# A two-layer cross network on one core: VectorE's order in layer 2, and a third buffer for layer 1's kept channels

## The chip, the cores and the metric

The kernel runs on one core of a Trainium2 chip. The metric is device microseconds from the first to the last instruction of one execution, the median of several runs. All data is float32.

## The reference, cut to what matters

```python
ROWS, FIELDS, EMB = 4096, 32, 16

def _batchnorm(h, gamma, beta):            # per channel, over rows and embedding
    mean = jnp.mean(h, axis=(0, 2), keepdims=True)
    var = jnp.var(h, axis=(0, 2), keepdims=True)
    return (h - mean) * jax.lax.rsqrt(var + EPS) * gamma[None, :, None] + beta[None, :, None]

def _cin_layer(out, x, W, b, gamma, beta):
    r, _, e = x.shape
    h = jnp.einsum('rne,rfe->rnfe', out, x).reshape(r, -1, e)   # all products of two fields
    h = jnp.einsum('rce,oc->roe', h, W) + b[None, :, None]      # 128 output channels
    return _batchnorm(h, gamma, beta)

h1 = _cin_layer(x, x, W1, b1, g1, beta1)         # 32 x 32 products
out, direct1 = (h1[:, :64], h1[:, 64:])
direct2 = _cin_layer(out, x, W2, b2, g2, beta2)  # 64 x 32 products
agg = jnp.concatenate([direct1, direct2], axis=1)
return agg.sum(axis=-1)
```

There are 4096 x 16 = 65,536 sites. For each, layer 1 multiplies fields by fields and contracts the products with `W1`; half of its channels are kept for layer 2, the other half goes to the output. Layer 2 multiplies the 64 kept channels by the 32 fields and contracts with `W2`. Batch norm needs statistics of all sites, so layer 2 starts only when layer 1 has ended.

## The kernel before

Sites are taken in tiles of 512 columns, and two tiles make a pair: 128 tiles, 64 pairs. **Layer 1**, tile by tile: VectorE multiplies (`z`), TensorE contracts into a PSUM bank, ScalarE copies the bank out with its bias, VectorE takes statistics. The kept channels of a pair are gathered in a tile `kept` and written to HBM:

```python
opool = one.enter_context(tc.tile_pool(name="opool", bufs=2))
# [...] in finish(t), for each tile t of pair c:
            if half == 0:
                eds[c] = epool.tile([P, T], FP, tag="ed", name="ed")
                kept[c] = opool.tile([KEEP, 2 * T], FP, tag="h", name="kept")
            e = opool.tile([P, T], FP, tag="e", name="e")
            nc.scalar.activation(e, ps, AF.Identity, bias=b1)
            stats1.add(e)
            h = kept[c]
            nc.scalar.activation(h[:, half * T : (half + 1) * T], ps[:KEEP, :], AF.Identity, bias=b1[:KEEP])
            if half == 1:
                nc.scalar.dma_start(hs[c], kept.pop(c))
```

The last two pairs of layer 1 first finish their kept half (L468 is the copy, L470 the statistics), so that the factors of layer 2 are known early; their direct half follows on TensorE behind it:

```python
        for c in range(NC - ENDING // 2, NC):
            add_halves(banks, zs, 0, ks, True, True)           # matmuls of the kept channels
            h = opool.tile([KEEP, 2 * T], FP, tag="h", name="kept")
            for half, k in enumerate(ks):
                # [...] copy out of PSUM on ScalarE, statistics on VectorE
            nc.scalar.dma_start(hs[c], h)
        # [...] mean, variance, root, scale and shift -> keep, by a small matmul into keep_ps
```

**Layer 2** takes a pair c in four stages k (i = 3, 0, 1, 2). In each, ScalarE makes two factors `f` in PSUM (kept channels, scaled and shifted), VectorE multiplies them with the fields `b` and `bx` into `zz`, and GpSimd makes sums `t` of the products. TensorE contracts both: the 2 x 2 blocks of channels and tiles are multiplied in a scheme that saves block products by such sums.

```python
psum = ctx.enter_context(tc.tile_pool(name="psum", bufs=6, space=bass.MemoryType.PSUM))
factors = ctx.enter_context(tc.tile_pool(name="factors", bufs=2, space=bass.MemoryType.PSUM))
z2pool = ctx.enter_context(tc.tile_pool(name="z2pool", bufs=3))   # zz
tpool = ctx.enter_context(tc.tile_pool(name="tpool", bufs=2))     # t
hpool = ctx.enter_context(tc.tile_pool(name="hpool", bufs=1))     # th

def sum_products(z):                     # stages 1 to 3, on GpSimd
    t = tpool.tile([P, 3, 2, T], FP, tag="t", name="t")
    queue("pool", lambda: nc.gpsimd.tensor_tensor(t[:, 0], z[:, 1], z[:, 0], ALU.add))             # L674
    twice = t[:, 0].unsqueeze(1).to_broadcast([P, 2, 2, T])
    queue("pool", lambda: nc.gpsimd.tensor_tensor(t[:, 1:3], z[:, 2:4], twice, ALU.subtract))      # L677
    return t
# sum_half(z, b11), stage 0: th = one add on VectorE, one subtraction on GpSimd (L685)
```

TensorE takes in each stage: `x1`, `x32`, then `x54` of the stage before, then `x67`; in the last stage its own `x54` at the end. `x67` reads t[:, 0], `x54` reads t[:, 1:3]. All matmuls of layer 2 go through line 669, and two of them, for the low and high 64 rows of a PSUM bank, run beside each other. A pair uses four of six banks: x11, x62, x34 and x57. When a pair's matmuls have ended, `combine` adds its banks up during the next pair's stages. It is a generator, and each `step()` records one section of it:

```python
    def combine(c, sums_):
        act(both[low], x11[high]); act(both[high], x11[low], bias=b2[low])      # ScalarE
        yield
        add(both, both, x11)                                                    # VectorE
        yield
        if idle:
            dve(idle.pop(0))              # statistics of layer 1's direct half, in the first pairs
        add(e[:, 0], both, x62)           # VectorE: e0
        yield
        act(u2[low], e[low, 0], ...); act(u2[high], e[low, 0], ...)             # ScalarE
        yield
        add(u3, u2, x57)                                                        # VectorE
        yield
        act(u3_low, u3[high])                                                   # ScalarE
        yield
        add(e[:, 1], u3, x34); add(e[low, 0], u3_low, x57[low])                 # VectorE: e1, e_low
        yield
        # [...] squares on ScalarE; in the first pair statistics on VectorE
        yield
        # [...] tensor_reduce d<-e on VectorE
        yield
```

The stage loop before:

```python
        for k, i in enumerate(STAGES):
            # [...]
            multiply(z[:, 0::3], f1, b)          # VectorE: zz<-f,b
            if k in (1, 2, 3):
                step()
            if c > 0 or k > 0:
                f2 = factor(raw[i], i, 1)        # ScalarE
                if k == 1:
                    step()
                # [...] stage 0: copy b11 on ScalarE
                multiply(z[:, 1:3], f2, bx)      # VectorE: zz<-f,bx
            # [...] t = sum_half(...) in stage 0, sum_products(z) else
            if k == 1:
                step()
            if k < 3:
                f1 = factor(raw[STAGES[k + 1]], STAGES[k + 1], 0)   # ScalarE, for the next stage
            if k == 0:
                step(2)
            if k == 2:
                step()
            # [...]
            if k == 1:
                step()
            # [...] the matmuls of the stage
        steps = combine(c, sums_)
```

VectorE, ScalarE, GpSimd and TensorE each keep the order in which their instructions are recorded here.

Of the kernel before, what the change touches and what calls it, by code (L numbers as in the profile page):

```python
# [38 lines left out]
FP = mybir.dt.float32  # L39
# [8 lines left out]
T = 512  # L48
# [3 lines left out]
KEEP = 64  # L52
# [16 lines left out]
def tile_cin(ctx: ExitStack, tc: tile.TileContext, xa, xb, xr, w1, w1m, w2, bn, out):  # L69
# [119 lines left out]
    def load_x(g, k):  # L189

        at = xb.offset + ((2 * DIFF * g + 1) * WRAP + 2 * k) * T
        nc.sync.dma_start(xs[:, k], bass.AP(xb.tensor, at, [[2 * WRAP * T, DIFF], [4 * T, 8], [1, 2 * T]]))

    def negate(part):
        x = xs[:, 0, part * T : (part + 1) * T]
        return nc.scalar.activation(x, x, AF.Identity, scale=-1.0)

    def difference(part):

        to = slice(part * T // 2, (part + 1) * T // 2)  # L200
        return nc.vector.tensor_reduce(xd[:, to], xs[:, :, to].rearrange("p k t -> p t k"), AX.X, ALU.add)

    def store_difference(g):
        return nc.scalar.dma_start(diffs[g], xd)
# [10 lines left out]
    def loaded(c):  # L215
        if c == 0:
            b, bx, *a = early[-6:]
        else:
            with tc.issue_after(loads[-1].ins):
                b, bx = load_b(c), load_bx(c)  # L220
                a = [load_a(c, i) for i in STAGES]
        return dict(zip(STAGES, a)), b, bx
# [3 lines left out]
    def queue(engine, make):  # L226

        with tc.issue_after(lasts[engine].ins) if engine in lasts else nullcontext():
            lasts[engine] = make()
        return lasts[engine]  # L230
# [30 lines left out]
    with ExitStack() as one:  # L261
        lpool = one.enter_context(tc.tile_pool(name="lpool", bufs=4))
        rpool = one.enter_context(tc.tile_pool(name="rpool", bufs=1))
        opool = one.enter_context(tc.tile_pool(name="opool", bufs=2))
        zpool = one.enter_context(tc.tile_pool(name="zpool", bufs=4))
        wpool = one.enter_context(tc.tile_pool(name="wpool", bufs=1))

# [49 lines left out]
        kept = {}  # L317

        def finish(t):

            c, half = divmod(t, 2)
            ps = pss.pop(t)
            to = slice(half * KEEP, (half + 1) * KEEP)
            if half == 0:
                eds[c] = epool.tile([P, T], FP, tag="ed", name="ed")
                kept[c] = opool.tile([KEEP, 2 * T], FP, tag="h", name="kept")
            ed = eds[c]
            e = opool.tile([P, T], FP, tag="e", name="e")
            nc.scalar.activation(e, ps, AF.Identity, bias=b1)  # L329
# [5 lines that stand above are left out]
            done = nc.scalar.activation(ed[to, :], ps[KEEP:, :], AF.Identity, bias=b1[KEEP:])  # L335
            if half == 1:
                sum_direct(c)
            return done

        def sum_direct(c):  # L340
            return nc.vector.tensor_reduce(
                d1[:, c * RT : (c + 1) * RT],
                eds.pop(c).rearrange("p (r e) -> p r e", e=EMB),
                AX.X,
                ALU.add,
            )
# [81 lines left out]
        def add_halves(banks, zs, direct, ks, begun, ended):  # L428

            for m in range(4):  # L430
                for k in ks:
                    matmul(
                        banks[k][half_of[(k + direct) % 2]],
                        w1_sb[:, m, half_of[direct]],
                        zs[k][:, m // 2, m % 2, :],
                        m == 0 and not begun,
                        m == 3 and ended,
                    )
# [20 lines left out]
        for c in range(NC - ENDING // 2, NC):  # L459
            ks = tuple(2 * c + half - ending for half in range(2))  # L460
            add_halves(banks, zs, 0, ks, True, True)
            h = opool.tile([KEEP, 2 * T], FP, tag="h", name="kept")
            for half, k in enumerate(ks):
                at = half_of[half]
                to = h[:, half * T : (half + 1) * T]
                bias = (b1, b1_swapped)[half][at]
                with tc.issue_after(evicted.ins):
                    queue("act", lambda: nc.scalar.activation(to, banks[k][at], AF.Identity, bias=bias))  # L468
                stats = stats1.more[low, 2 * k : 2 * k + 2].rearrange("p a b -> p (a b)")
                queue("dve", lambda: nc.vector.bn_stats(stats, to))  # L470
            nc.scalar.dma_start(hs[c], h)
# [324 lines left out]
    def step(count=1):  # L796
        for _ in range(count):
            next(steps, None)

    for c in range(NC):  # L800
        raw, b, bx = loaded(c)
        sums_ = Sums()
        g = c // DIFF + 1
        if g < NC // DIFF:
            if c % DIFF == 2:
                with tc.issue_after(loads[-1].ins):
                    for k in range(2):
                        load_x(g, k)
            if c % DIFF == 4:
                for k in range(2):  # L810
                    queue("act", lambda: negate(k))
                idle += [lambda k=k: difference(k) for k in range(4)]
            if c % DIFF == 13:
                queue("act", lambda: store_difference(g))

        f1 = factor(raw[STAGES[0]], STAGES[0], 0)
        for k, i in enumerate(STAGES):

            z = z2pool.tile([P, 4, 2, T], FP, tag="zz", name="zz")
            if c == k == 0:  # L820

                f2 = factor(raw[i], i, 1)
                for q in range(2):
                    multiply_part(z[:, 0::3], f1, b, q)
                    multiply_part(z[:, 1:3], f2, bx, q)
                b11 = factors.tile([P, T], FP, tag="f", name="b11")
                act(b11, z[:, 0, 1])
            else:
                multiply(z[:, 0::3], f1, b)
            if k in (1, 2, 3):  # L830

                step()
            if c > 0 or k > 0:
                f2 = factor(raw[i], i, 1)
                if k == 1:
                    step()
                if i == PLAIN:
                    b11 = factors.tile([P, T], FP, tag="f", name="b11")
                    act(b11, z[:, 0, 1])
                multiply(z[:, 1:3], f2, bx)  # L840

            plain = (0,) if i == PLAIN else (0, 1) if c == 0 and k == 3 else ()
            if i == PLAIN:
                t = sum_half(z, b11)
            elif not plain:
                t = sum_products(z)
            if k == 1:
                step()
            if k < 3:
                f1 = factor(raw[STAGES[k + 1]], STAGES[k + 1], 0)  # L850
            if k == 0:
                step(2)
            if k == 2:

                step()
            for _ in range(min(len(sums_left), 4 if c == NC - 1 else 1)):
                queue("act", sums_left.pop(0))
            if k == 1:
                step()

            low_first = c % 2 == 0
            rest = not low_first
            last = range(8) if k == 3 else ()
            if c == 0 and k > 1:
                last = ((0, 1, 6, 7), (2, 3, 4, 5))[k - 2]
            stage = Stage(sums_, i, z, t, plain, last)
            if i == PLAIN:
                stage.ordinary(low_first, 0)
            if len(plain) == 2:
                stage.ordinary(rest, 0)  # L870
            else:
                stage.x1(low_first if i == PLAIN else rest)
                stage.x32(rest)
            if k > 0:
                waiting.x54(rest)
            if len(plain) == 2:
                stage.ordinary(rest, 1)
            else:
                stage.x67(rest)
                if k == 3:  # L880
                    stage.x54(rest)
            waiting = stage

            if c == 9 and k == 2:
                queue("act", direct_factors)
            if 10 <= c < 14 and k == 2:
                queue("act", lambda: scale_direct(c - 10))
            if c == 15 and k == 2:
                with tc.issue_after(loads[-1].ins):
                    write_direct()  # L890
        steps = combine(c, sums_)
# [90 lines left out]
```

## Time and profile before

| | |
|---|---|
| time, median of 3 runs | 2090.25 us (2089.69 to 2091.75) |
| span of the profiled run | 2088.1 us |
| layer 1 | to 476 us |
| change of layers, first layer 2 pair | 476 to about 520 us |
| layer 2 | to 2071 us, then 17 us to the end |
| one multiplication zz on VectorE | 2.27 us, eight in a pair |
| one first sum t (L674), one second sum (L677) on GpSimd | 2.37 and 4.56 us, three of each in a pair |
| one th sum on GpSimd (L685) | 2.37 us |
| `both`, e, u on VectorE | 0.67 to 0.69 us each |

In the profile, PE is TensorE, PEld its weight loads, DVE VectorE, ACT ScalarE, POOL GpSimd and SP SyncE. A matmul in float32 shows as two records. A wait is written as the engine and line that waited, and what released it. A timeline line gives start, duration, engine, line, operation and tiles; in brackets is the idle time before it and what ended it. Tile names are cut to their stem: `x` stands for the four banks of layer 2, `u` for u2 and u3, `e` for all parts of e. A wait for several things is put down to the one that came last.

### The profile page before, as it was taken

What the parts mean: (1) busy time and instruction counts of PE and PEld (TensorE: products, weight loads), DVE (VectorE), ACT (ScalarE), POOL (GpSimd) and SP (SyncE); (2) the same over time, 40 slices, a digit from 0 to 9 for tenths busy, and PEclk for the clock granted to TensorE, in tenths of its full rate; (3) what the DMA queues carried; (4) which work ended last, traced back from release to release, by engine and by line L of the source; (5) the groups of instructions that cost most, each with busy time, mean ns of one, the idle gap of its engine ahead of it and who ended that gap; (6) DMA issues with size and microseconds to landing.
All of it is one profiled execution on the core that took longest, in us unless ns stands there. A gap on an engine that the chain in (4) does not pass through costs nothing.

```text
span 2088.1 us, 23629 instructions
## 1 busy us (share of the span) xinstructions
PE 2066.8 (99%) x8634; PEld 1024.2 (49%) x8634; DVE 1890.0 (91%) x1391; ACT 1008.3 (48%) x1594; POOL 1472.0 (70%) x453
## 2 busy tenths in 40 slices
PE   9999999999999999999999999999999999999996
PEld 3444444443343555555555555555555555555553
DVE  8998888888999999899999998999999989999996
ACT  4555555554454444445444445454444454444443
POOL 0000000003999999999999999999999999999995
PEclk9999999999999999999999999999999999999998
DMA  9999999997666787776677777766667777667751
GB/s 384 390 335 345 335 363 352 350 337 193 162 168 165 172 195 189 192 176 166 166 188 173 185 174 176 172 169 162 170 168 183 177 174 178 169 165 168 171 142 41
DMA packets 112020, 440.65 MB, mean 211 GB/s; under 512 B 13088, under 2 KB 13088, under 8 KB 103456
## 3 DMA queue, kind: packets, MB, share of 16 engines
q1 hardware_dynamic: 105456, 418.43, 73.3%
q10 hardware_dynamic: 6448, 20.72, 2.6%
q8 instruction: 67, 1.10, 0.2%
q14 instruction: 49, 0.40, 0.1%
HBM read 417.07 MB, written 22.02 MB: 210 GB/s over the span
## 4 chain that ended last, share of the span: by engine, by line
PE 94%; DVE 2%; POOL 1%; issue 1%; DMA 1%; ACT 1%; DVEq 0%; SPq 0%; ACTq 0%; POOLq 0%
PE x L669 72%; PE ps L397 21%; PE ps L358 2%; DVE zz L638 1%; POOL t L677 0%; DMA h<-kept 0%; POOL t L674 0%; DMA b<-in_xb 0%; ACT f L630 0%; DVE zz L643 0%; DVE e L633 0%; ACT both L630 0%; DVE d L912 0%; ACT unread L568 0%; ACT u L630 0%
## 5 line engine op out<-in xcount | busy, mean ns | idle before, releaser
L669 PE MATMUL x<-zz,s_sb 128*64 128x512 f32 x2048 | 946.3, 592 | 0.3 <-DVE zz L638 0.3
L669 PE MATMUL x<-zz,w_sb 128*64 128x512 f32 x2312 | 889.9, 592 | 0.0
L677 POOL TENSOR_TENSOR t<-zz,t 128x2048 f32<-128x2048 f32 x191 | 870.7, 4559 | 15.0
L669 PE MATMUL x<-t,s_sb 128*64 128x512 f32 x1528 | 694.2, 593 | 0.1
L630 ACT ACTIVATE f<-a,keep 128x512 f32<-128x512 f32 x512 | 398.0, 778 | 415.2 <-DVE zz L638 371.5
L638 DVE TENSOR_TENSOR zz<-f,b 128x2048 f32<-128x2048 f32 x255 | 580.6, 2277 | 0.1
L638 DVE TENSOR_TENSOR zz<-f,bx 128x2048 f32<-128x2048 f32 x255 | 579.9, 2274 | 0.0
L674 POOL TENSOR_TENSOR t<-zz 128x1024 f32<-128x1024 f32 x191 | 453.2, 2373 | 89.6 <-DVE zz L638 80.0
L685 POOL TENSOR_TENSOR th<-zz,th 128x1024 f32<-128x1024 f32 x64 | 151.8, 2373 | 487.4 <-DVE th L633 487.3
L397 PE MATMUL ps<-z,w_sb 128*128 128x512 f32 x992 | 434.2, 595 | 0.6 <-DVE z L365 0.6
L669 PEld LDWEIGHTS x<-zz,s_sb 128*64 128x64 f32 x2048 | 279.6, 137 | 228.6 <-issue 159.1
L669 PEld LDWEIGHTS x<-zz,w_sb 128*64 128x64 f32 x2312 | 306.0, 137 | 164.5 <-issue 75.7
L669 PE MATMUL x<-t,w_sb 128*64 128x512 f32 x764 | 360.8, 594 | 0.9 <-POOL t L677 0.9
L365 DVE TENSOR_TENSOR z<-a,b 128x2048 f32<-128x2048 f32 (+1 forms) x129 | 293.1, 2273 | 55.4 <-PE ps L397 45.1
L669 PEld LDWEIGHTS x<-t,s_sb 128*64 128x64 f32 x1528 | 206.4, 137 | 230.3 <-issue 184.2
L397 PEld LDWEIGHTS ps<-z,w_sb 128*128 128x128 f32 x992 | 185.8, 190 | 247.0 <-issue 239.8
L329 ACT ACTIVATE e<-ps,bn_sb 128x512 f32<-128x512 f32 x124 | 85.2, 687 | 224.3 <-PE ps L397 211.5
L630 ACT ACTIVATE u<-e,bn_sb 64x512 f32<-64x512 f32 x64 | 46.3, 723 | 219.1 <-DVE e L633 219.1
L669 PE MATMUL x<-th,s_sb 128*64 128x512 f32 x256 | 130.7, 592 | 0.0
L633 DVE TENSOR_TENSOR both<-both,x 128x512 f32<-128x512 f32 x64 | 44.0, 688 | 94.6 <-ACT both L630 94.6
L669 PEld LDWEIGHTS x<-t,w_sb 128*64 128x64 f32 x764 | 101.6, 137 | 52.0 <-issue 13.6
L669 PE MATMUL x<-zz,neg_sb 128*64 128x512 f32 x264 | 124.0, 592 | 0.0
(104 smaller groups left out, 1230.2 us busy)
## 6 DMA issues: line engine op xcount, KB each, us to landing
a<-h SPq DMA_DIRECT2D x256, 512.0 KB, 5.7
a<-in_xa SPq DMA_DIRECT2D x128, 512.0 KB, 6.4
b<-in_xb SPq DMA_DIRECT2D x128, 512.0 KB, 7.3
b<-in_xb SPq DMA_DIRECT2D x64, 1024.0 KB, 8.8
bx<-in_xb SPq DMA_DIRECT2D x64, 512.0 KB, 7.7
bx<-x SPq DMA_DIRECT2D x64, 512.0 KB, 9.3
h<-kept ACTq DMA_DIRECT2D x64, 256.0 KB, 5.8
r<-in_xr SPq DMA_DIRECT2D x16, 512.0 KB, 7.7
```

The source lines that it names most:

```text
L329: nc.scalar.activation(e, ps, AF.Identity, bias=b1)
L358: nc.tensor.matmul(pss[t + k], w1_sb[rows, 4 + t % GROUP // 4, :], zr[rows, :], start=not ended, stop=ended)
L365: return nc.vector.tensor_tensor(z[:, k], a.rearrange("p (a t) -> p a t", a=2)[:, k].unsqueeze(2).to_broadcast([P, n, 2, T]), b.rearrange( ...
L397: nc.tensor.matmul(pss[t], w1_sb[:, m, :], z[:, m // 2, m % 2, :], start=(t == m == 0), stop=(t > 0 and m == 3))
L630: return queue("act", lambda: nc.scalar.activation(to, source, AF.Identity, **scale_bias))
L633: return dve(lambda: nc.vector.tensor_tensor(to, x, y, ALU.add))
L638: dve(lambda: nc.vector.tensor_tensor(z, a, b.rearrange("p (k q) t -> p k q t", k=2), ALU.mult))
L669: queue("pe", lambda: nc.tensor.matmul(self.of[x], w, b, start=start, stop=stop))
L674: queue("pool", lambda: nc.gpsimd.tensor_tensor(t[:, 0], z[:, 1], z[:, 0], ALU.add))
L677: queue("pool", lambda: nc.gpsimd.tensor_tensor(t[:, 1:3], z[:, 2:4], twice, ALU.subtract))
L685: queue("pool", lambda: nc.gpsimd.tensor_tensor(t[:, 1:3, 0], z[:, 2:4, 1], twice, ALU.subtract))
```

## The change

In layer 2, sections of `combine` are recorded elsewhere in the stage loop: every VectorE addition (or pair of additions) of it now stands behind one multiplication of the next pair. It is meant to let VectorE multiply while ScalarE and TensorE prepare what the addition needs. In layer 1 the tile `kept` gets a pool of its own with three buffers, so that a new tile need not wait for the write of the one but one before.

```diff
         opool = one.enter_context(tc.tile_pool(name="opool", bufs=2))
+        kpool = one.enter_context(tc.tile_pool(name="kpool", bufs=3))
 [...]
-                kept[c] = opool.tile([KEEP, 2 * T], FP, tag="h", name="kept")
+                kept[c] = kpool.tile([KEEP, 2 * T], FP, tag="h", name="kept")
 [...]
-            h = opool.tile([KEEP, 2 * T], FP, tag="h", name="kept")
+            h = kpool.tile([KEEP, 2 * T], FP, tag="h", name="kept")
 [...]
                 multiply(z[:, 0::3], f1, b)
-            if k in (1, 2, 3):
+            if k > 0:
                 step()
             if c > 0 or k > 0:
                 f2 = factor(raw[i], i, 1)
-                if k == 1:
+                if k == 2:
                     step()
 [...]
-            if k == 1:
+            if k in (1, 2):
                 step()
             if k < 3:
                 f1 = factor(raw[STAGES[k + 1]], STAGES[k + 1], 0)
-            if k == 0:
-                step(2)
-            if k == 2:
+            if k < 3:
                 step()
             for _ in range(min(len(sums_left), 4 if c == NC - 1 else 1)):
                 queue("act", sums_left.pop(0))
-            if k == 1:
-                step()
```

With "zz(k,b)" for a multiplication of stage k, VectorE's order over a pair's beginning is

| before | th, both, zz(1,b), e0, zz(1,bx), u3, zz(2,b), e1, e_low, zz(2,bx), zz(3,b), d, ... |
|---|---|
| after | th, zz(1,b), both, zz(1,bx), e0, zz(2,b), u3, zz(2,bx), e1, e_low, zz(3,b), d, ... |

## The prediction

> **What bounds the kernel now.** I read the engine shares first, then the stretches of the run, then the list of waits, and last the timelines of single pairs. The page gives the shares:
>
> ```profile
> PE 2066.8 (99%) x8634; PEld 1024.2 (49%) x8634; DVE 1890.0 (91%) x1391; ACT 1008.3 (48%) x1594; POOL 1472.0 (70%) x453
> ```
>
> TensorE looks full, but a busy share of a pipelined engine hides short gaps, so I count records instead. The busy times by stretch:
>
> ```profile
> 476.00:493.00 17.00, 16.01 (x84) 5.11 (x78) 11.03 (x22) 7.61 (x13) 0.00 (x0) 1.00 0.73 207
> 569.00:2071.00 1502.00, 1501.86 (x6962) 788.56 (x6962) 1380.00 (x936) 719.62 (x1141) 1406.15 (x428) 1.00 0.70 169
> ```
>
> In the timeline of undisturbed matmuls the record starts stand 0.2146 us apart (1200.10 to 1208.04 is 37 steps in 7.94 us). The 6962 records of the long stretch then need 6962 x 0.2146 = 1494 us of its 1502. So in steady layer 2 **about 8 us can be had at most**, 0.13 us in each of the 61 pairs; a pair of 114 records needs 24.46 us and takes 24.6. The layer 1 stretch repeats every 15.0 us, set by TensorE, and the last 17 us after the final matmul are a chain of their own. What TensorE waits for in layer 2 stands in the waits:
>
> ```profile
> POOL t L674 <- DVE zz L638: 80.0, 64, 5.3
> PEld x L669 <- POOL t L677: 25.8, 64, 1.8
> DVE e L633 <- PE x L669: 23.7, 24, 2.7
> POOL t L674 <- PE x L669: 9.6, 23, 0.5
> ACT kept L468 <- DMA h<-kept: 3.3, 1, 3.3
> ```
>
> Columns are total us, times, longest. Once per pair TensorE's weight load waits for GpSimd's second sum t (L677): it is that of the pair's last stage, whose two products are the last of the pair. GpSimd in turn waits once per pair for a VectorE multiplication zz. So the question is what sets the start and the end of GpSimd's row of sums. Its timeline over one pair boundary:
>
> ```profile
> 1201.63 2.37 POOL L674 TENSOR_TENSOR t<-zz 128x1024 f32<-128x1024 f32 x1 [0.41 <-PE x L669]
> 1204.08 4.56 POOL L677 TENSOR_TENSOR t<-zz,t 128x2048 f32<-128x2048 f32 x1
> 1208.60 2.36 POOL L685 TENSOR_TENSOR th<-zz,th 128x1024 f32<-128x1024 f32 x1
> 1212.35 2.38 POOL L674 TENSOR_TENSOR t<-zz 128x1024 f32<-128x1024 f32 x1 [1.39 <-DVE zz L638]
> ```
>
> The sum ending at 1208.64 lets TensorE go on at 1208.69. The next row could start at 1210.96, but starts 1.39 us later, because the second multiplication of stage 1 is late. Why, VectorE's timeline of the same time tells:
>
> ```profile
> 1205.49 0.69 DVE L633 TENSOR_TENSOR both<-both,x 128x512 f32<-128x512 f32 x1 [1.53 <-ACT both L630]
> 1206.09 2.29 DVE L638 TENSOR_TENSOR zz<-f,b 128x2048 f32<-128x2048 f32 x1
> 1209.32 0.69 DVE L633 TENSOR_TENSOR e<-both,x 128x512 f32<-128x512 f32 x1 [0.94 <-PE x L669]
> 1209.92 2.29 DVE L638 TENSOR_TENSOR zz<-f,bx 128x2048 f32<-128x2048 f32 x1
> ```
>
> VectorE is in order: it stands 1.53 us for ScalarE's copy before `both`, and 0.94 us for TensorE before the first `e`, with the multiplication that GpSimd needs behind both.
>
> **What the Trainium skill says.** "Perfetto Trace Analysis", section "Identifying the Most-Contended Engine", warns that matmul busy share does not measure the distance to the limit; agreed: 99% here, with 8 us between records. The same page, "Optimization Strategy", says that the same gap repeating on the engine that should be full can mean too few buffers for the next tile. The trace has both kinds: in 23 pairs GpSimd's third L674 waits for TensorE (9.6 us together), to free one of two t tiles; in the others it is late by VectorE. "SBUF — State Buffer", section "SBUF: two separate sides", says that a VectorE operation with two SBUF inputs locks GpSimd out. The multiplications read f from PSUM, so should not; L677's spread of 4523 to 4590 ns agrees.
>
> **The change, part by part.** No instruction is added or taken away on a compute engine; they move. TensorE's order stays; VectorE's becomes th, zz(1,b), both, zz(1,bx), e0, zz(2,b), u3, zz(2,bx), e1, e_low, zz(3,b), d, and so on. ScalarE makes the factor of stage 2 before the two `u` copies, and the load of b goes one place earlier in the SyncE queue.
>
> (a) *Early pairs.* In the first pairs VectorE also has statistics to do, so the delay is largest. The chain that ended last goes there through VectorE:
>
> ```profile
> 544.51 0.62 DVE direct_stats L612
> 545.13 0.65 DVE e L633
> 545.78 2.21 DVE zz L638
> 548.13 2.39 POOL t L674
> ```
>
> It ends in TensorE going on at 569.14, after a stop of 1.5 us. By hand with the new order: th ends 540.34, the factor is ready at 540.36, zz(1,b) takes 540.4 to 542.7, `both` to 543.3 (its copies are done at 541.67), zz(1,bx) to 545.5. GpSimd starts at 545.6 in place of 548.13, 2.5 us earlier. TensorE's t-tile release then holds the last stage, so that 0.1 us remains of the 1.5: gain 1.4. By the same step the pair before, which takes 24.95 us against the settled 24.58 between starts of like records, gains 0.4. The pairs after these two are 0.03 to 0.2 us over the settled period (24.73, 24.79, 24.70), together 0.5. **Sum 2.3 us.**
>
> (b) *Settled pairs.* New order from 1203.16, the end of zz(0,bx): th ends 1203.96, zz(1,b) 1204.05 to 1206.3, `both` to 1206.9 (copies done 1205.45, no wait left), zz(1,bx) to 1209.1 in place of 1212.20. GpSimd starts at 1210.96, straight after th, 1.39 earlier. But two sums later it meets the other limit: the third L674 needs the t tile that TensorE frees at 1201.63 + 24.5 = 1226.1; it ran at 1226.29 before. Then 2.37 + 4.56 + 0.08 follow, and L677 ends at 1233.1 in place of 1233.27. Of 1.39 us only **0.1 to 0.2 is left**, in every second pair; the pairs between them stand at the tile release already. The weight load of the products has to be there one slot ahead, so not all of 0.17 comes back: I take 0.08 x 30 = **2.4 us**. About 0.1 us per pair stays lost, because the chain from that release (7.0 us and two semaphores) is just longer than TensorE's 36 records in between (7.7 us less pipeline depth and preloading).
>
> (c) *kept with three tiles.* At the end of layer 1:
>
> ```profile
> 480.09 0.68 ACT L468 ACTIVATE kept<-ps,bn_sb 64x512 f32<-64x512 f32 x1 [2.63 <-PE ps L426]
> 484.77 0.68 ACT L468 ACTIVATE kept<-ps,bn_sb 64x512 f32<-64x512 f32 x1 [3.29 <-DMA h<-kept]
> ```
>
> The second waits for a write of 7.9 us that began at 476.78. Not all of 3.29 us is this: the matmuls that it also needs, 16 records in concurrent halves at 0.43 us per two, end 8 x 0.43 = 3.43 us after those of the first, at 483.5. So 1.25 us are gained; then statistics, factors and the first multiplication follow one another. TensorE is occupied up to 487.9 with direct halves, and the small matmul of the factors came at 488.94, so 1.1 to 1.2 can move. **Gain 1.2 us.** In the rest of layer 1 kept is not waited for.
>
> Sum: 2.3 + 2.4 + 1.2 = 5.9 us. I take off 0.2 for what the new order delays (a choice): 2090.25 - 5.7 is about **2084.5 us**.
>
> **The rivals.** *A PSUM bank takes over.* The next pair's x57 goes into the bank of x62, which e0 reads; e0 now stands behind one more multiplication. By (b) it would end at about 1209.9, as before (1210.01), and TensorE needs the bank at 1211.3; if VectorE ran 1.5 us later than by hand, each pair would pay. A loss of 0.2 us per pair would be 12 us: 2097. VectorE's idle time of 1.9 us per pair speaks against. *The t tiles hold everything.* Then (b) gives nothing and (a) and (c) remain: 2087. The 23 waits for TensorE speak for it. *GpSimd's lead frees TensorE wholly:* all 8 us and (c) come: 2081. Against it stand pairs that wait at the t tile already and are no shorter. *SyncE's new order* delays an input: loads land in 5.7 to 9.3 us and have most of a 24.6 us pair, so it should stay hidden.
>
> **Range and chances.** The bound of 8 us (which holds most of (a)), plus 1.2 and 0.4 of the pair before the stretch, puts the floor near 2080.5; 2% would be 41.8 us, four times that. Slower by 2% needs 0.65 us more in every pair, which no wait above is near. I set 2081 to 2088.5.
>
> **What would show it.** The wait of kept for its DMA is gone (right for (c)) and the first layer 2 matmul stands about 1.2 us earlier. VectorE's waits for `both` and e fall; GpSimd's 80 us wait for zz falls to under 10, and its 9.6 us wait for TensorE grows to over 60, in nearly all pairs. The stop of 1.5 us before 569 is gone. The period settles between 24.50 and 24.58. Wrong would be: a wait of TensorE for VectorE's e that grows, GpSimd still late by zz, or a period at 24.46.

## The result and the profile after

The changed kernel takes 2084.36 us (median of 6 runs, 2084.07 to 2086.47) against 2090.98 us for the kernel before in the same comparison: a ratio of **0.9969, with a 95% interval of 0.9957 to 0.9982**. That is 6.6 us, within 2%. The profiled spans, 2088.1 and 2082.0 us, differ by 6.1 us.

First the page and the busy times by stretch of the kernel after. In the second, a group is busy us and records of PE, PEld, DVE, ACT and POOL, then the granted clock.

```profile
PE 2061.8 (99%) x8634; PEld 927.9 (45%) x8634; DVE 1901.4 (91%) x1391; ACT 998.9 (48%) x1594; POOL 1471.8 (71%) x453
```

```profile
569.00:2065.00 1496.00, 1496.00 (x6954) 689.42 (x6950) 1387.16 (x932) 709.04 (x1140) 1403.38 (x426) 1.00 0.72 169
```

TensorE's share still reads 99%. But 6954 records at 0.2146 us would need 1492.3 us, and the stretch takes 1496: 3.7 us are lost there, where the kernel before lost 8. The waits of the kernel after (engine and line, releaser: us in total, times, longest):

```profile
POOL t L675 <- PE x L670: 78.9, 63, 1.7
PEld x L670 <- POOL t L678: 41.4, 158, 0.9
DVE e L634 <- PE x L670: 27.6, 49, 2.6
DVE both L634 <- ACT both L631: 14.0, 30, 5.7
POOL t L675 <- DVE zz L639: 5.0, 2, 2.8
```

Line numbers are one higher than before, and shift by another line or two in some of the experiments. GpSimd waited for VectorE's products 64 times and 80.0 us; now twice and 5.0 us. Instead it waits for TensorE 63 times, once in each pair but one: the wait has changed hands. The second line stood at 25.8 us before, and has grown although TensorE loses less. It does not measure the loss: in this trace TensorE's weight loads start two by two, and many of them have some 0.23 us of idle time ahead of them whether or not a sum is late. Where GpSimd's wait sits, its timeline of one pair shows (two sums between the second and the third line are left out):

```profile
1204.23 2.38 POOL L686 TENSOR_TENSOR th<-zz,th 128x1024 f32<-128x1024 f32 x1
1206.56 2.40 POOL L675 TENSOR_TENSOR t<-zz 128x1024 f32<-128x1024 f32 x1
1216.01 4.58 POOL L678 TENSOR_TENSOR t<-zz,t 128x2048 f32<-128x2048 f32 x1
1221.80 2.37 POOL L675 TENSOR_TENSOR t<-zz 128x1024 f32<-128x1024 f32 x1 [1.21 <-PE x L670]
1224.25 4.56 POOL L678 TENSOR_TENSOR t<-zz,t 128x2048 f32<-128x2048 f32 x1
```

The row of sums now starts right behind th, without the old wait of 1.39 us, and then loses 1.21 us ahead of its last stage, waiting for a free tile t. VectorE's timeline of the same pair:

```profile
1223.57 2.29 DVE L639 TENSOR_TENSOR zz<-f,b 128x2048 f32<-128x2048 f32 x1 [0.35 <-PE x L670]
1225.78 0.68 DVE L634 TENSOR_TENSOR both<-both,x 128x512 f32<-128x512 f32 x1
1226.37 2.28 DVE L639 TENSOR_TENSOR zz<-f,bx 128x2048 f32<-128x2048 f32 x1
1228.99 0.69 DVE L634 TENSOR_TENSOR e<-both,x 128x512 f32<-128x512 f32 x1 [0.33 <-PE x L670]
```

`both` no longer waits for ScalarE here (14.0 us in the whole run, 94.6 before). e0 still waits for TensorE, but nothing that GpSimd needs soon stands behind it. A wait of VectorE for TensorE ahead of a multiplication is new, 0.35 us in the first line. It costs nothing: the version with the split tile, in which TensorE loses nothing in the settled pairs, has it too (46.8 us in all).

Where the 6.1 us of the profiled runs come from, by the start of like records in both traces (for a pair, the median of its records' starts):

| | before | after | gained in this part |
|---|---|---|---|
| first layer 2 matmul | 492.83 | 492.52 | 0.31 |
| pair 1 | 532.84 | 532.53 | 0.00 |
| pair 3 | 583.79 | 581.51 | 1.97 |
| pair 12 | 805.50 | 802.19 | 1.03 |
| pair 63 | 2059.27 | 2053.03 | 2.93 |
| end | 2088.14 | 2082.00 | -0.10 |

From pair 12 on, the period from pair to pair is 24.584 us before and 24.526 us after. 114 records at 0.2146 us are 24.46.

### The profile page after: what moved, and what is told of

It is laid out like the page before. It is cut to its first block, busy times and chain, and to the rows that moved or that the text cites. A ratio compares the mean times of both kernels' runs of the same rounds, so it can differ in the third digit from the quotient of the medians.

```text
span 2082.0 us, 23630 instructions
## 1 busy us (share of the span) xinstructions
PE 2061.8 (99%) x8634; PEld 927.9 (45%) x8634; DVE 1901.4 (91%) x1391; ACT 998.9 (48%) x1594; POOL 1471.8 (71%) x453
## 4 chain that ended last, share of the span: by engine, by line
PE 75%; DVE 1%; ACT 0%; DVEq 0%; issue 0%; ACTq 0%
PE x L670 75%; DVE zz L644 0%; DVE zz L639 0%; DVE e L634 0%; DVE d L911 0%; ACT u L631 0%; DVE d L779 0%; ACT f L631 0%; DVEq L977 0%; DVE u L634 0%; DVE groups_x L774 0%; DVE groups L774 0%; ACT sd L139 0%; DVE mv L136 0%; DVE ss L157 0%
## 5 line engine op out<-in xcount | busy, mean ns | idle before, releaser
L631 ACT ACTIVATE f<-a,keep 128x512 f32<-128x512 f32 x512 | 393.2, 776 | 283.3 <-DVE zz L639 281.1
L670 PEld LDWEIGHTS x<-zz,w_sb 128*64 128x64 f32 x2312 | 290.9, 137 | 251.1 <-issue 250.1
L569 ACT ACTIVATE unread<-e,center 128x512 bf16<-128x512 f32 x124 | 89.7, 724 | 120.4 <-DVE e L634 118.6
```

Source lines behind the costliest of these rows:

```text
L569: return nc.scalar.activation(unread, e[:, s], AF.Square, bias=center[:, s], accum_out=squares[:, s, c : c + 1])
L631: return queue("act", lambda: nc.scalar.activation(to, source, AF.Identity, **scale_bias))
L670: queue("pe", lambda: nc.tensor.matmul(self.of[x], w, b, start=start, stop=stop))
```

## The experiments

Each ran against the kernel before on its own chip, which took 2090.16 us in the first set, 2090.03 in the second and 2090.90 in the third. Times of different sets are therefore compared through the ratio, and differences under 1 us through the traces.

### Each half of the change alone

Layer 1's part only, on the kernel before:

```diff
+        kpool = one.enter_context(tc.tile_pool(name="kpool", bufs=3))
-   ... opool.tile([KEEP, 2 * T], FP, tag="h", name="kept")     # twice
+   ... kpool.tile([KEEP, 2 * T], FP, tag="h", name="kept")
```

> Layer 1's part alone: kept with three tiles, layer 2's order as before. Theory 1 (the traces: the second copy of kept starts 1.25 us earlier, but the factors of layer 2 start only 0.3 us earlier, because ScalarE has two copies of the direct half ahead of them): 0.3 us faster than before, about 2090. Rival (the chain of statistics is what counts, as predicted): 1.2 us faster, about 2089. First layer 2 matmul at 492.5 by the first, 491.6 by the second.

Measured: 2089.75 us, ratio 0.9998 (0.999 to 1.0006): not to be told from none. From the small matmul of the factors to the first layer 2 matmul it takes 4.64 us, against 3.89 before and 4.65 after. The small matmul itself comes about 1.1 us earlier in the kernel after (487.87 against 488.94), so 0.76 us of it is lost again on the way. (The first layer 2 matmul stands at 492.06 here, because this run's layer 1 began earlier as a whole.)

Layer 2's order only, the reverse edit on the kernel after:

> Layer 2's order alone, kept with two tiles. Theory 1: nearly the whole gain, 5.8 us faster than before, 2084.7; settled period 24.53 us, the two early stops of TensorE gone. Rival (the third tile of kept is worth 1.2 us): 2085.5, 5 us faster.

Measured: 2084.05 us, ratio 0.997 (0.9959 to 0.9982), period 24.524 us. The order is the whole measurable gain.

### Where kept's gain went: ScalarE's order

ScalarE's timeline of the kernel after, at the change of layers:

```profile
483.52 0.68 ACT L469 ACTIVATE kept<-ps,bn_sb 64x512 f32<-64x512 f32 x1 [2.04 <-PE ps L427]
487.96 0.69 ACT L512 ACTIVATE ed<-ps,bn_sb 64x512 f32<-64x512 f32 x1 [1.09 <-PE ps L427]
488.67 0.68 ACT L512 ACTIVATE ed<-ps,b_swapped 64x512 f32<-64x512 f32 x1
489.26 1.48 ACT L631 ACTIVATE f<-a,keep 128x512 f32<-128x512 f32 x2
```

The second kept copy starts 1.25 us earlier than before (484.77), as the prediction says. But two copies of pair 62's direct half (`ed`, L512) are queued ahead of the factors f, and they wait for TensorE's direct half until 487.96. So the factors start at 489.26, though what they need (`keep`) is there at 488.46. In the kernel before the same two copies cost nothing, for the second of them ended at 489.52, when `keep` (489.53) was only just there:

```profile
488.84 0.68 ACT L511 ACTIVATE ed<-ps,b_swapped 64x512 f32<-64x512 f32 x1
```

The edit, on the kernel after, puts the factors first:

```diff
                 if c < NC - 1:
-                    queue("act", evict)
+                    first_evictions.append(evict)
 ...
         raw, b, bx = loaded(c)
+        if c == 0:
+            f1, f2 = (factor(raw[STAGES[0]], STAGES[0], half) for half in range(2))
+            for make in first_evictions:
+                queue("act", make)
```

> As after, but ScalarE makes the first two factors of layer 2 ahead of the two copies of the direct half of pair 62 (1.4 us). Theory 1 (these copies took what the third tile of kept had gained): the first multiplication of layer 2 at 489.3 in place of 490.06, first layer 2 matmul at about 491.8, 0.7 us faster than after: 2083.7. Rival (TensorE's direct half, which ends at 491.25 anyway, or the copies themselves, which release two PSUM banks, set the start): no gain, or some tenths slower.

Measured: 2083.21 us, ratio 0.9968 (0.9956 to 0.998). The time alone does not separate it from after (0.9969); the trace does:

```profile
488.30 1.48 ACT L632 ACTIVATE f<-a,keep 128x512 f32<-128x512 f32 x2 [1.63 <-DVE keep L504]
489.81 0.68 ACT L513 ACTIVATE ed<-ps,bn_sb 64x512 f32<-64x512 f32 x1
```

The factors now wait for `keep` alone. The first multiplication starts at 489.12 in place of 490.06 (0.19 us of this is an earlier small matmul in this run), and from the small matmul to the first layer 2 matmul it is 3.89 us again: 0.76 us came back.

### Which of the two waits mattered

Two waits stood ahead of GpSimd's input: e0 for TensorE (23.7 us in all) and `both` for ScalarE, in the kernel before:

```profile
DVE both L633 <- ACT both L630: 94.6, 64, 4.9
```

Each was moved alone, in the kernel after, so that kept's third tile is in both runs. First e0 only, `both` staying ahead of stage 1's first multiplication:

```diff
-            if k > 0:
+            if k > 1:
                 step()
 ...
             if k < 3:
-                step()
+                step(2 if k == 0 else 1)
```

> As after, but `both` stands ahead of stage 1's first multiplication, as before; e0 stays behind the second multiplication. Theory 1 (what counts is that no wait for TensorE's x62 stands before GpSimd's input): by hand `both` at 1205.5, multiplications to 1210.5, just before th ends at 1210.96, so GpSimd starts as in after: 2084 to 2085, period 24.53, GpSimd's wait for zz under 15 us. Rival (the larger wait of the two, 94.6 us of `both` for ScalarE, is what was worth moving): half of the gain or less, 2087 or more.

Measured: 2084.76 us, ratio 0.9973 (0.9963 to 0.9983), period 24.515. Against 2084.05 of the order alone on the same chip it keeps all but 0.7 us. VectorE's wait for `both` is even longer than before:

```profile
DVE both L634 <- ACT both L631: 114.2, 64, 5.1
```

GpSimd's wait for zz is 19.8 us in 13 pairs, a little over what was expected; that is in the early pairs, where pair 2 to pair 3 takes 25.06 us against 24.52 after. Then `both` only, e0 ahead of the second multiplication as before:

```diff
-            if k > 0:
-                step()
+            if k > 0:
+                step(2 if k == 1 else 1)
             # [...] u3, e1 at their places of before
```

> As after, but only `both` moves behind stage 1's first multiplication; e0 stays ahead of the second one, and u3, e1 as before. Theory 1 (e0's wait for TensorE holds the second multiplication at its old place in every second pair): settled pairs gain nothing, period 24.57 to 24.59, GpSimd's wait for zz stays over 50 us; only kept and some of the early pairs come: 2088 to 2089.5. Rival (`both` was the costly wait): most of the gain, 2085 to 2086.

Measured: 2088.52 us, ratio 0.9992 (0.9985 to 0.9998), period 24.587. VectorE's timeline says why:

```profile
1202.35 2.29 DVE L639 TENSOR_TENSOR zz<-f,b 128x2048 f32<-128x2048 f32 x1
1204.56 0.68 DVE L634 TENSOR_TENSOR both<-both,x 128x512 f32<-128x512 f32 x1
1207.57 0.69 DVE L634 TENSOR_TENSOR e<-both,x 128x512 f32<-128x512 f32 x1 [2.33 <-PE x L670]
1208.17 2.28 DVE L639 TENSOR_TENSOR zz<-f,bx 128x2048 f32<-128x2048 f32 x1
```

VectorE's wait for `both` fell from 94.6 to 4.9 us, and its wait ahead of e0 grew from 23.7:

```profile
DVE e L634 <- PE x L670: 103.8, 63, 2.7
```

The multiplication behind e0 stays where it was. The larger sum of waiting was the one not worth moving: the wait that ends last decides.

### The tile t holds the rest

The tile was cut in two, in the same memory, so that the first sum needs only the release by `x67`, and the second sum that by `x54`:

```diff
-        t = tpool.tile([P, 3, 2, T], FP, tag="t", name="t")
-        queue("pool", lambda: nc.gpsimd.tensor_tensor(t[:, 0], z[:, 1], z[:, 0], ALU.add))
+        ta = tpool.tile([P, 2, T], FP, tag="ta", name="ta")
+        t = tpool.tile([P, 2, 2, T], FP, tag="t", name="t")
+        queue("pool", lambda: nc.gpsimd.tensor_tensor(ta, z[:, 1], z[:, 0], ALU.add))
```

> As after, with the tile t cut in two, one for the first sum and one for the second, two buffers each, the same memory. The first sum then needs only the release by x67, 20 records earlier than x54's. Theory 1 (the 0.06 us per pair that after still loses over 24.464 is the chain from the release of the t tile by x54 through 7.0 us of sums): the first sum no longer waits 1.2 us for TensorE, the second ends over 1 us before TensorE needs it, period 24.46 to 24.47, 3.5 us faster than after: about 2081. Rival (the rest belongs to TensorE itself, to the way that its two halves follow one another, or to VectorE): period 24.52 and 2084.4 as after.

Measured: 2080.45 us, ratio **0.9955 (0.9942 to 0.9967)**, period 24.462 us in the trace. GpSimd's timeline:

```profile
1211.67 4.55 POOL L679 TENSOR_TENSOR t<-zz,ta 128x2048 f32<-128x2048 f32 x1
1216.18 2.37 POOL L676 TENSOR_TENSOR ta<-zz 128x1024 f32<-128x1024 f32 x1
1219.75 4.55 POOL L679 TENSOR_TENSOR t<-zz,ta 128x2048 f32<-128x2048 f32 x1 [1.20 <-PE x L670]
```

The first sum of the last stage follows the sum before at once; the wait for TensorE, as long as ever (1.20 us), now stands between the two sums, with 2.37 us less work behind it. TensorE no longer waits for the last second sum: its period is that of its records.

The same edit on the kernel before:

> The kernel before, with the tile t cut in two as in the other run. Theory 1 (before is held by VectorE's lateness in every second pair, by the tile in the rest): only the pairs held by the tile gain, period 24.50 to 24.57, 1 to 4 us faster than before, 2086 to 2089, and GpSimd goes on waiting for zz. Rival (the tile alone held all pairs, and the new order of VectorE brought nothing by itself): about as fast as after with the split tile, 2081 to 2083.

Measured: 2090.18 us, ratio 1.0003 (0.9995 to 1.0011). Nothing, less than either theory expected.

```profile
1212.00 2.38 POOL L675 TENSOR_TENSOR ta<-zz 128x1024 f32<-128x1024 f32 x1 [1.76 <-DVE zz L638]
```

GpSimd still waits for VectorE. In most of this trace the pairs alternate: the stop at the end is small or gone in one, and in the next it has grown. The periods go as far apart as 24.46 and 24.75 us, and are 24.580 in the mean from pair 12 on. So the pairs that the tile seemed to hold took their share of one delay by VectorE over two pairs: without the tile's wait, the same delay falls on the other pair.

### The bank of e0

The rival of the prediction, that TensorE comes to wait for the PSUM bank that e0 reads, was to be provoked by putting e0 and all behind it one multiplication later:

```diff
-            if k in (1, 2):
+            if k == 2:
                 step()
 ...
-            if k < 3:
+            if k in (0, 2):
                 step()
+            if k == 3:
+                step(2)
```

> As after, but e0 and all sections behind it one multiplication later. Theory 1 (x57 of the next pair takes over the PSUM bank that e0 reads, and TensorE needs it 1.3 us after e0 ends now): e0 ends 2.2 us later, so TensorE stands about 1 us in each pair: 60 us slower than after, 2130 to 2160, with a wait of TensorE for e of 50 us or more. Rival (VectorE starts earlier by the same time, since fewer waits stand in its way, and the bank is never late): within 5 us of after.

Measured: 2086.83 us, ratio 0.9984 (0.9978 to 0.9991). My theory of 60 us fell; the rival's "within 5 us" held as a number. The settled period is 24.526, as after. But the rival's reason does not hold: VectorE is not earlier by the same time, e0 comes 1.8 to 2.8 us later against TensorE, about as the theory said. What the theory had wrong is the bank. In the pair looked at, x57's first record starts at 1210.53 and e0 ends only at 1210.67, and from pair 1 on x57 starts before e0's end in every pair, by up to 4.8 us. As x57's matmuls write over what is in their bank, they can't be in the bank that e0 still reads. TensorE's wait shows which ones are:

```profile
PE x L670 <- DVE e L634: 2.1, 2, 1.8
550.53 1.04 PE L670 MATMUL x<-zz,w_sb 128*64 128x512 f32 x3 [1.82 <-DVE e L634]
```

The second line is the first record of `x1` in pair 2, the 17th of the pair, and e0 ends at 550.39, just ahead of it. So the bank is taken over some 12 records later than I had thought. In a settled pair that leaves some 2 us of room (1210.67 to 1212.72); in pairs 1 and 2, where VectorE has its statistics to do, TensorE does stand for the bank. The stop in pair 2 is 2.0 us of what the run loses: from pair 1 to pair 2 it takes 26.90 us in place of 24.46.

### Split tile and factors first together

> As after, with the split tile t and the first factors ahead of the two copies, the two edits that each gained alone. Theory 1 (they act in different stretches, and after the start TensorE is full): gains add, 1.0 us at the start and 3.9 us in the settled pairs, so 2079.4 to 2079.8, first layer 2 matmul at about 491.6, period 24.46. Rival (an earlier start is lost again, because the first pairs are bound by VectorE and inputs): 2080.4 as with the split tile alone.

Measured: **2079.42 us, ratio 0.9945 (0.9931 to 0.9959)**, period 24.462. This is 11.5 us under the kernel before on the same chip, and the lowest ratio of all versions; but against the split tile alone (0.9955) the intervals overlap, so that the two gains add is not shown by the times. The profiled run is the slowest of five (2080.24), and it shows why the start gains less in it: 4.45 us from the small matmul to layer 2, whose first matmul stands at 492.54 and not at 491.6.

```profile
490.08 1.23 DVE L645 TENSOR_TENSOR zz<-f,b 128x1024 f32<-128x1024 f32 x1 [1.40 <-DMA h<-kept]
```

The first multiplication waits for the write of the last kept tile, issued at 485.17. With the factors early, this write is next in line; in the profile of the factors first alone the multiplication did not yet wait for it. That it is reuse of layer 1's memory by layer 2's tiles is argued from the order of pools and was not tried.

## Why the prediction was right, and where it was not

The time was foretold at 2084.5 us with a range of 2081 to 2088.5; 2084.36 was measured. The gain was foretold as 5.7 us from 2090.25; the medians differ by 6.6 us, from 2090.98, and the profiled runs by 6.1. By its own steps:

- *The ceiling.* 8 us lost in settled layer 2 was right: with the split tile the period is 24.462 us, the 24.46 that came out of record starts. The floor of the range was added up wrongly. The stop of 1.5 us ends at 569.14, so it and the pair before it lie ahead of the stretch from 569, and the 8 us hold only 0.5 of the 2.3 us of (a), not most of it. 8 + 1.4 + 0.4 + 1.2 is 11.0 us, a floor near 2079; the version with the split tile and the factors first gained 11.5 us, more than the floor of 2080.5 allows.
- *(a) Early pairs, 2.3 us.* Right. Pairs 1 and 2 gained 0.49 and 1.49 us (0.4 and 1.4 foretold). Pairs 3 to 11 gained 1.03, of which 9 x 0.058 = 0.52 is the settled gain, which leaves 0.5 as foretold.
- *(b) Settled pairs, 2.4 us.* The mechanism was right and the term too small: 0.058 us in each of some 60 pairs is 3.5 us. I let every second pair gain 0.08 and the others nothing, because they stood at the tile release already. But both kinds lost the same before: by record starts, the pairs from 12 to 61 in which GpSimd waited for the tile lost 0.117 us each at their end, the others 0.126, and all of them 0.064 after. They were not independent: the split tile in the kernel before shows that one delay by VectorE was shared by two pairs in turn. The tile does cap the gain, as foretold, at 24.526. What stays open is a detail: the last second sum ends as late against TensorE as it did in the tile-held pairs before (7.67 us before and 7.68 after from the start of the record that released the tile, in the median), and yet the stop costs about 0.05 us less. In those pairs before, the records of the two halves started evenly 0.21 us apart; after, two by two. No run separated this.
- *(c) kept, 1.2 us.* This step failed. The 1.25 us at ScalarE's copy came as worked out, and 1.07 us reached the small matmul, but only 0.31 us the first layer 2 matmul. The sentence that statistics, factors and the first multiplication follow one another left out ScalarE's queue: two copies of the direct half, 1.4 us, stand between. With the factors ahead of them, 0.76 us came back.
- The miss in (c) of 0.9 us and the miss in (b) of 1.1 us nearly cancel, and so do a gain that was 0.9 us larger than foretold and a kernel before that was 0.7 us slower in the comparison. The closeness of the total is partly luck.
- *Signs.* GpSimd's wait for zz under 10 us and its wait for TensorE over 60 came true, so did the vanished stop of 1.5 us and the period. Two did not: the first layer 2 matmul 1.2 us earlier, and a falling wait for e, which rose from 23.7 to 27.6 us in a place where it costs nothing.
- *Rivals.* The bank did not take over. But the reading on which this rival was weighed, that x57 follows e0 in its bank, did not hold: with e0 later still, the matmuls that waited for it were those of x1. In the kernel after, too, x57 starts 0.5 us before e0 ends in pair 2; which matmuls follow e0 there in the settled pairs, its trace does not tell. The t tiles hold the remainder, not everything. SyncE's order did change the loads: those of `a` in layer 2 took 8.3 us from issue to landing in the median, 5.7 before, but no wait for a load shows in layer 2 after.

## What to carry to other kernels

Put an addition that waits behind work that a neighbour needs, and choose by which wait ends last ahead of that work, not by which has the larger total: here, with kept's third tile in both, moving the 94.6 us wait alone brought 1.6 us, moving the 23.7 us wait alone 5.4. When the late engine has been put right, look at what its neighbour waits for next; here it was a tile written by two instructions and held by the later reader, and cutting it in two cost no memory. A wait removed on an in-order engine helps only as far as nothing else with a wait of its own stands between in that queue, as the copies of the direct half did.

## What was not expected of the hardware

The same cut of the tile was worth nothing before the reordering (ratio 1.0003), and after it about 3 us by the ratios (0.9969 to 0.9955), 4 us by the spans of the traces. And the granted clock (0.996 to 0.997) and the matmul busy share (99%) are the same in all of these kernels, from 2079 to 2090 us: they do not tell them apart, the distance of record starts does.
